# A graph network's update step without row means, its result kept in PSUM, and three more groups of rows copied on the chip

## The chip, the cores and the metric

The kernel runs on one core of one Trainium2 chip. A core has a matrix engine (PE, with its weight loads shown apart as PEld), a vector engine (DVE), an activation engine (ACT), a general engine (POOL) that here issues gathers, and SP, which issues most other DMAs. Each works through its own queue in order; semaphores tie them together. The metric is the device time of one execution in microseconds (us). Three runs of the kernel before the change gave 2449.85, 2456.73 and 2466.41 us; their median is 2456.73 us.

## What is computed

One layer of a message-passing graph network over 12,500 nodes (64 features) and 200,000 edges (32 features, sorted by target node), then a residual and a normalisation of each row:

```python
msg_in = concatenate([nodes[row], nodes[col], edge_features])      # 200000 x 160
messages = relu(msg_in @ mW1 + mb1) @ mW2 + mb2
aggregated = segment_sum(messages, col, num_segments=12500)
upd = relu(concatenate([nodes, aggregated]) @ uW1 + ub1) @ uW2 + ub2
y = x + upd
out = (y - mean(y)) / sqrt(var(y) + 1e-5)                          # over the 64 features
```

Here `row` is the random source of an edge (`src`) and `col` its sorted target (`dst`).

## The kernel before

**Tables and tiles.** The first part of the run computes two tables in DRAM: A, every node's features times the source part of `mW1`, and B, the same for the target part. Edges are worked in tiles of 128; 6 tiles make a step (261 steps), 12 make a super block (131, number g). All values are 32-bit floats.

**One step s** of the main loop is written out by hand; this order is the order of every engine's queue. `edge_part` (L379) multiplies, on PE, a selection matrix and the edge features `l` with `rhs`, which holds a window of 32 rows of B and the weights of the edge features, into PSUM (`pc`, two buffers that rotate). `node_part` adds the gathered rows of A on DVE (L405, or L402) and applies relu on ACT (L406, or L403), giving `h`. One step later `collect` counts the edges per target (`cnt`, L435) and sums `h` per target (`sums`, L438) on PE, both in PSUM over a window that a register names. Every second step, `select` builds on DVE the selection for the next super block: it compares target numbers with first nodes (L250) and with slot numbers (L256). The slot numbers and the first nodes lie in PSUM, in a tile `cps` of 272 columns; the first nodes of 80 super blocks fit and are computed by `first_nodes`.

**Source rows.** For most tiles POOL gathers 128 rows of A by an indirect DMA (L218), up to nine steps ahead (`rows`, nine buffers). For two of the six tiles of some groups, the "copied" ones (a list `COPIED` made from `PACE`, 105 groups), the rows come from the transposed x that lies in SBUF: two tiles' 128 columns are copied one by one, half by ACT (L350, `singly`) and half by DVE (L357, `joined`), and PE multiplies them with the weights (L382). The address of a copy stands in two registers, which the engine loads first (L327), up to 16 words, for 8 columns, at once. The copies of a group are spread over the steps ahead of its own: DVE's share of a step falls into two or three parts (`share`) between its large operations, ACT's into one at the end of the step.

**Updates.** A run of steps whose targets span fewer than 448 nodes makes a period (34 of them, `UPD`). Its `sums` and `cnt` have 480 columns. When it ends, `close` copies them to SBUF (L453 ACT, L452 DVE), `carry` adds the 32 columns of overlap to the next period, `update` multiplies with the weights (`pu`, L475 and L476, in a `pc` buffer), `activated` applies relu (L481, ACT, at the end of the step), and a step later `residual` (L489, L491) computes y = x + update of four blocks of 128 nodes into `py`, which takes a `pc` buffer too. In the following steps, ACT copies y to SBUF (`evacuate`, L497), DVE takes statistics block by block (L505, L507), ACT a square root (L512), DVE a reciprocal and four subtract-and-multiply operations (L518, L521), and SP stores the rows (L529).

Of the kernel before, what the change touches and what calls it, by code (L numbers as in the profile page):

```python
# [10 lines left out]
F32 = mybir.dt.float32  # L11
# [6 lines left out]
P = 128  # L18
# [24 lines left out]
BS = 11  # L43
UB = 4
NCOL = (-(-N // P) + UB) * P
UN = 448
UW = UN + WIN
ONE = D - 1
LS = 8
# [21 lines left out]
U8 = mybir.dt.uint8  # L71
YBASE = XBASE + 4 * XCOLS
LEAD = 8
PACE = ((11, 0.42), (50, 0.446), (130, 0.429), (261, 0))
FINAL = 258


# [26 lines left out]

UPD = updates()

NODES = 80
UL = min(UB * P, -(-int(N * (1 - (UPD[-1] * SUB * P / E) ** 2) + WIN // 2) // 64) * 64)


# [1 line left out]
def gnn_kernel(ctx: ExitStack, tc: tile.TileContext, x1T, x, eT, e_rows, src, src_row, dst, dst_row, wlist, wrow, wnext, whalf,  # L112
# [54 lines left out]
    uz = const.tile([P, DH], F32, name="uz")  # L167
    ub1_s = const.tile([DH, 1], F32, name="ub1_s")
    u2 = const.tile([DH, D], F32, name="u2")
    ux = const.tile([P, D], F32, name="ux")  # L170
    w2u = const.tile([DH, DH], F32, name="w2u")
    ident = const.tile([P, P], F32, name="ident")
# [50 lines left out]
    with tc.tile_pool(name="sup", bufs=2) as sup, tc.tile_pool(name="work", bufs=2) as work, tc.manual_schedule():  # L223
# [13 lines left out]
        def first_nodes(a, b):  # L237

            c = WIN + SUP // 2 * (a % NODES)
            nc.vector.tensor_scalar(cps[:, c:c + SUP // 2 * (b - a)], wh[:, SUP // 2 * a:SUP // 2 * b], pidx, None, op0=ALU.add)  # L240

        def select(g, at=None):


            nt = min(SUP, NT - g * SUP)
            l = L[g]
            c = WIN + SUP // 2 * (g % NODES)
            node = cps[:, c:c + SUP // 2]
# [7 lines left out]
            nc.vector.tensor_tensor(s[:, :nt], slot.unsqueeze(1).broadcast_to([P, nt, WIN]),  # L256
                                    drc[:, g * SUP:g * SUP + nt].unsqueeze(2).broadcast_to([P, nt, WIN]),
                                    op=ALU.is_equal)
            S[g] = s
# [201 lines left out]
        def blocks(u):  # L461
            return UB if u + 1 < K else -(-UL // P)
# [21 lines left out]

        def residual(u):

            py = psum.tile([P, UB, D], F32, name="py", tag="sums" if u + 2 == K else "pc")
            for i in range(blocks(u)):
                nc.tensor.matmul(py[:, i], xw[u % 2][:, i * P:(i + 1) * P], ux, start=i == 0, stop=False)  # L489
            for i in range(blocks(u)):  # L490
                nc.tensor.matmul(py[:, i], hT[:, i * P:(i + 1) * P], u2, start=False, stop=i + 1 == blocks(u))  # L491
            ys[u] = py

        def evacuate(u):

            y = work.tile([P, UB, D], F32, name="y")
            nc.scalar.copy(y, ys[u])  # L497
            ys[u] = y

        def statistics(u):  # L500

            st = work.tile([P, UB, nc.vector.BN_STATS_DIM], F32, name="st")
            mv = work.tile([P, UB, nc.vector.BN_AGGR_DIM], F32, name="mv")
            for i in range(blocks(u)):
                nc.vector.bn_stats(out=st[:, i], in_=ys[u][:, i])  # L505
            for i in range(blocks(u)):
                nc.vector.bn_aggr(out=mv[:, i], in_=st[:, i])  # L507
            mvs[u] = mv

        def deviation(u):  # L510
            sd = work.tile([P, UB], F32, name="sd")
            nc.scalar.activation(sd[:, :blocks(u)], mvs[u][:, :blocks(u), 1], AF.Sqrt, bias=eps)  # L512
            sds[u] = sd

        def norm(u):
            y, mv, sd = ys.pop(u), mvs.pop(u), sds.pop(u)
            rs = work.tile([P, UB], F32, name="rs")
            nc.vector.reciprocal(rs[:, :blocks(u)], sd[:, :blocks(u)])  # L518
            o = work.tile([P, UB, D], F32, name="y") if u + 1 == K else y
            for i in range(blocks(u)):  # L520
                nc.vector.tensor_scalar(o[:, i], y[:, i], mv[:, i, 0:1], rs[:, i:i + 1],  # L521
                                        op0=ALU.subtract, op1=ALU.mult)
            us[u] = (us[u], o)

        ys, mvs, sds = {}, {}, {}
# [153 lines left out]
        def rest(s):  # L679
# [4 lines left out]
                zeros(s - 3, 8)  # L684
            if s == 6:
                first_nodes(8, NODES)
            if s == 2 * NODES - 3:
                first_nodes(NODES, NSUP)
            if s == 9:
                columns_list()  # L690
            if s == 1:
# [35 lines left out]

        def checks():

# [34 lines left out]
        at_end = {n: [(evacuate, K - 3), (statistics, K - 3)], n + 1: [(deviation, K - 3), (norm, K - 3), (store, K - 3)],  # L764
                  n + 2: [(stage, K - 2) for stage in (evacuate, statistics, deviation, norm, store)]}

        period = [max(u for u in range(K) if UPD[u] <= s) for s in range(NSUB)]
        transpose(0)
# [3 lines left out]
        for s in range(last + 2):  # L772
# [48 lines left out]
            if due.get(s) == K - 1:  # L821
                activated(K - 1)
                residual(K - 1)
                statistics(K - 1)
                deviation(K - 1)
            if s + 2 in due and due[s + 2] + 1 < K:
# [15 lines left out]

    flag = nc.values_load(flag_i[0:1, 0:1], min_val=0, max_val=2 * EBULK,
# [167 lines left out]
```

## Time and profile before

| | us |
|---|---|
| median of three runs | 2456.73 |
| lowest, highest | 2449.85, 2466.41 |
| the profiled execution | 2450.92 |
| its span, first to last instruction | 2449.1 |

The profile is of one execution, 0.24% under the median. Its page counts an engine as busy while an instruction works; loading registers, waiting on semaphores and issuing DMAs are not counted, and stand as idle time, either under the name of what ended the wait or as "issue", when nothing visible was waited for. "Remote" is a release that the trace ascribes to no instruction. In the rows of groups the columns are line, engine, operation, output and input, shapes and number; then busy us and mean ns of one; then the idle us just before them and what ended most of it. The granted clock of PE has a mean of 0.555 in this run.

### The profile page before, as it was taken

Reading aid. Unit: us, or ns where it says so; the run is one execution under the profiler, and the core shown is the slowest. Engines: PE = TensorE matmul, PEld = TensorE weight load, DVE = VectorE, ACT = ScalarE, POOL = GpSimd, SP = SyncE. Lnnn points to the kernel's source line nnn. Section 1 sums busy time; section 2 is a strip of 40 time slices with the busy share of each in tenths; the row PEclk is TensorE's granted clock in tenths of the full one; section 3 lists DMA queues with packets and bytes.
Section 4 is the critical chain, followed back from the end, with each engine's and each line's share of the span. In section 5 each row is a group of like instructions: output and inputs, shape, how many; then the busy total and the mean of one; then the engine's idle time right before and its main releaser. Section 6 shows DMA issues by size and latency. Waiting matters only on the chain.

```text
span 2449.1 us, 47549 instructions
## 1 busy us (share of the span) xinstructions
PE 1612.1 (66%) x9656; PEld 1381.8 (56%) x9656; DVE 1125.1 (46%) x7813; ACT 1603.2 (65%) x7158; POOL 1278.5 (52%) x1362
## 2 busy tenths in 40 slices
PE   1247566666657665666666667576667777878878
PEld 1236455555546554655555556565555665656767
DVE  0212544444545444444454454544454454445554
ACT  0005666667877776767776777676777777767773
POOL 7254555555555555555555555555555555545550
PEclk9956555555555555555555555555555555555556
DMA  5343232332222222222222232322222233223332
GB/s 133 102 119 97 75 81 77 83 84 64 75 69 71 74 64 70 72 66 74 69 71 77 71 82 73 80 75 76 78 74 77 73 83 80 72 73 80 81 81 53
DMA packets 207165, 191.50 MB, mean 78 GB/s; under 512 B 57211, under 2 KB 173265, under 8 KB 206881
## 3 DMA queue, kind: packets, MB, share of 16 engines
q0 software_dynamic: 43296, 86.79, 14.3%
q1 hardware_dynamic: 149040, 92.72, 13.7%
q10 hardware_dynamic: 14546, 8.93, 1.3%
q8 instruction: 91, 1.49, 0.3%
q14 instruction: 192, 1.57, 0.2%
HBM read 170.52 MB, written 17.76 MB: 77 GB/s over the span
## 4 chain that ended last, share of the span: by engine, by line
issue 27%; PE 18%; ACT 12%; DVE 12%; POOL 12%; another core or an unknown queue 8%; DMA 3%; DVEq 3%; ACTq 2%; SPq 1%; POOLq 0%
POOL xg L218 12%; ACT xc L350 10%; PE sums L438 7%; DVE xc L357 6%; PE pc L379 6%; DVEq L327 3%; DVE h L405 2%; ACTq L327 2%; PE py L489 1%; PE py L491 1%; DVE pc L402 1%; DVE l L250 1%; SPq L287 1%; DMA xg<-tab_a,src_s 1%
## 5 line engine op out<-in xcount | busy, mean ns | idle before, releaser
L218 POOL DMA_INDIRECT xg<-tab_a,src_s x1293 | 1220.7, 944 | 1086.5 <-DVE h L405 427.7
L350 ACT ACTIVATE xc<-xtop,xbot 128x1 f32 x6720 | 1321.7, 281 | 342.4 <-issue 319.7
L357 DVE TENSOR_TENSOR xc<-xtop,xbot 128x1 int32 x6720 | 608.5, 154 | 723.1 <-issue 701.8
L438 PE MATMUL sums<-sel,h 128*128 128x32 f32 x3126 | 686.1, 385 | 208.9 <-issue 71.5
L438 PEld LDWEIGHTS sums<-sel,h 128*128 128x128 f32 x3126 | 653.4, 312 | 239.1 <-issue 71.6
L379 PE MATMUL pc<-rhs,l 64*128 64x128 f32 x3126 | 477.4, 434 | 284.1 <-issue 77.3
L379 PEld LDWEIGHTS pc<-rhs,l 64*128 64x128 f32 x3126 | 389.4, 307 | 357.5 <-issue 182.6
L435 PEld LDWEIGHTS <-one 128*1 128x1 bf16 x1563 | 63.6, 83 | 219.6 <-issue 209.6
L406 ACT ACTIVATE h<-h 128x768 f32<-128x768 f32 x147 | 121.7, 828 | 83.9 <-DVE h L405 76.5
L405 DVE TENSOR_TENSOR h<-pc,xg 128x768 f32<-128x768 f32 x147 | 139.4, 949 | 65.8 <-PE pc L379 18.8
L435 PE MATMUL cnt<-sel,one 128*1 128x32 bf16 x1563 | 107.5, 188 | 82.3 <-issue 82.0
L250 DVE TENSOR_TENSOR l<-l,cps 128x768 f32<-128x768 int32 (+1 forms) x134 | 127.2, 949 | 67.9 <-DMA l<-in_dst_row 51.5
L403 ACT ACTIVATE h<-pc 128x768 f32<-128x768 f32 x105 | 84.1, 801 | 103.0 <-DVE pc L402 84.3
L402 DVE TENSOR_TENSOR pc<-pc,xg 128x512 f32<-128x512 f32 x105 | 73.4, 699 | 146.4 <-remote 57.9
L256 DVE TENSOR_TENSOR sel<-cps,drc 128x384 f32<-128x384 f32 x131 | 72.0, 549 | 113.3 <-PE sums L438 75.6
L382 PE MATMUL pc<-w1a,xc 64*128 64x128 f32 x420 | 89.5, 405 | 6.9 <-issue 6.9
L382 PEld LDWEIGHTS pc<-w1a,xc 64*128 64x128 f32 x420 | 79.1, 317 | 8.2 <-issue 8.1
L594 ACT COPY tb<-pb 128x512 f32<-128x512 f32 (+1 forms) x13 | 7.4, 569 | 114.0 <-remote 73.6
L584 PE MATMUL pb<-w1a,xtop 64*128 64x128 f32 x100 | 23.5, 413 | 86.7 <-DVE tb L592 62.0
L489 PE MATMUL py<-ux,xw 128*128 128x64 f32 x268 | 62.4, 410 | 27.3 <-remote 22.1
L489 PEld LDWEIGHTS py<-ux,xw 128*128 128x128 f32 x268 | 56.6, 311 | 34.9 <-remote 23.0
L433 PE MATMUL cnt<-zero_b 128*1 128x480 bf16 x34 | 18.6, 547 | 81.2 <-DVE xw L452 47.4
(103 smaller groups left out, 844.3 us busy)
## 6 DMA issues: line engine op xcount, KB each, us to landing
l<-in_dst_row SPq DMA_DIRECT2D x262, 96.0 KB
l<-in_eT SPq DMA_DIRECT2D x262, 96.0 KB
xg<-tab_a,src_s POOLq DMA_INDIRECT x1293
rhs<-tab_b SPq DMA_DIRECT2D x361, 32.0 KB
tab_b<-tb SPq DMA_DIRECT2D x13, 512.0 KB
rhs<-tab_b SPq DMA_DIRECT2D x387, 16.0 KB
tab_a<-tb ACTq DMA_DIRECT2D x12, 512.0 KB
out<-y SPq DMA_DIRECT2D x33, 128.0 KB
```

What stands on the lines that cost most here:

```text
L218: nc.gpsimd.indirect_dma_start(out=a[:, i, :] if s < XG else a[:, i // 2, i % 2, :], out_offset=None, in_=A[:, :] if s >= XG else x[:, :], ...
L250: nc.vector.tensor_tensor(l[r], l[r].bitcast(I32), node[r].unsqueeze(2).broadcast_to([r.stop - r.start, SUP // 2, P]), op=ALU.is_equal)
L327: _, v = nc.values_load_multi_w_load_instructions(col_a[k % P:k % P + 1, k // P].rearrange("k e b -> k (e b)")[:, 2 * a:2 * m], engines=[e ...
L350: nc.scalar.activation(o[:, e:e + 1], top.bitcast(F32), AF.Identity, bias=bot.bitcast(F32))
L357: nc.vector.tensor_tensor(o[:, e:e + 1].bitcast(I32), top.bitcast(I32), bot.bitcast(I32), op=ALU.bitwise_or)
L379: nc.tensor.matmul(pc[:, b, k, :], L[g][q:q + 64, m, :], rhs[g % 2][q:q + 64, w, :], start=s >= XG or k == 0, stop=s >= XG and not copied)
L382: nc.tensor.matmul(pc[:, b, k, :], xc[s][q:q + 64], w1a[q:q + 64], start=False, stop=True)
L405: nc.vector.tensor_tensor(h[:, b, :m], pc[:, b, :m], a[:, b, :m], op=ALU.add)
L406: nc.scalar.activation(h[:, b, :m], h[:, b, :m], AF.Relu)
L435: nc.tensor.matmul(pn[:, bass.ds(ws[i], WIN)], one, SB[g][:, k0 + i, :, 1], start=False, stop=ends and i == n - 1)
L438: nc.tensor.matmul(ps[:, bass.ds(ws[i], WIN)], h[:, i % 2, i // 2, :], S[g][:, k0 + i, :], start=False, stop=ends and i == n - 1)
L489: nc.tensor.matmul(py[:, i], xw[u % 2][:, i * P:(i + 1) * P], ux, start=i == 0, stop=False)
```

## The change

Five things change together.

- **No row means.** The weights behind y, `u2` and `ux`, get each row's mean over the 64 outputs subtracted (into `u2c` and `ux`, once, on DVE), so that y has a mean of zero in every row. Statistics shrink to a sum of squares.
- **y stays in PSUM.** `residual` writes into a fixed part of the tile `cps` (now 384 columns: 32 slot numbers, 96 first nodes, 256 for y) in place of a `pc` buffer. ACT's copy goes; ACT writes the squares to SBUF instead, at the end of the step of the residual, one step before the copy stood. DVE sums them with one reduction in place of eight statistics operations, ACT takes the root of the scaled sum, and one multiplication on DVE, reading y from PSUM, replaces four operations. Every stage and the store come one step earlier. First nodes of 32 super blocks fit; `select` computes the next ones when they are used up.
- **DVE's copies by whole loads.** `share` splits a step's copies at multiples of four pairs of columns, so that parts begin with full loads of 16 words.
- **Updates of 480 nodes.** `UN` is 480, sums and counts have 512 columns, and there are 32 periods.
- **108 copied groups.** `PACE` rises from 0.446 to 0.459 between steps 50 and 130 and from 0.429 to 0.442 after.

```diff
-UN = 448
+UN = 480
-PACE = ((11, 0.42), (50, 0.446), (130, 0.429), (261, 0))
+PACE = ((11, 0.42), (50, 0.459), (130, 0.442), (261, 0))
-NODES = 80
+NODES = 32
+YC = WIN + NODES * SUP // 2
...
-    cps = cpool.tile([P, WIN + NODES * SUP // 2], F32, name="cps")
+    cps = cpool.tile([P, YC + UB * D], F32, name="cps")
...
+            if g and g % NODES == 0:
+                first_nodes(g, min(g + NODES, NSUP))
...
         def share(todo, part, of):
-            n = -(-len(todo) // of)
-            todo = todo[part * n:part * n + n]
+            c = CHUNK // 2
+            n = max(int(len(todo) / of / c + 0.5), 1) * c
+            todo = todo[part * n:(part + 1) * n if part + 1 < of else None]
...
         def residual(u):
-            py = psum.tile([P, UB, D], F32, name="py", tag="sums" if u + 2 == K else "pc")
+            py = cps[:, YC:].rearrange("p (i d) -> p i d", d=D)
...
-                nc.tensor.matmul(py[:, i], hT[:, i * P:(i + 1) * P], u2, start=False, stop=i + 1 == blocks(u))
+                nc.tensor.matmul(py[:, i], hT[:, i * P:(i + 1) * P], u2c, start=False, stop=i + 1 == blocks(u))
...
-        def evacuate(u):
-            y = work.tile([P, UB, D], F32, name="y")
-            nc.scalar.copy(y, ys[u])
-            ys[u] = y
+        def squares(u):
+            n = blocks(u)
+            sq = work.tile([P, UB, D], F32, name="y")
+            nc.scalar.activation(sq[:, :n], ys[u][:, :n], AF.Square)
+            sqs[u] = sq
...
         def statistics(u):
-            for i in range(blocks(u)):
-                nc.vector.bn_stats(out=st[:, i], in_=ys[u][:, i])
-            for i in range(blocks(u)):
-                nc.vector.bn_aggr(out=mv[:, i], in_=st[:, i])
+            nc.vector.tensor_reduce(ss[:, :n], sqs.pop(u)[:, :n], AX.X, ALU.add)
...
-            nc.scalar.activation(sd[:, :blocks(u)], mvs[u][:, :blocks(u), 1], AF.Sqrt, bias=eps)
+            nc.scalar.activation(sd[:, :n], ss[:, :n], AF.Sqrt, bias=eps, scale=1.0 / D)
...
-            for i in range(blocks(u)):
-                nc.vector.tensor_scalar(o[:, i], y[:, i], mv[:, i, 0:1], rs[:, i:i + 1],
-                                        op0=ALU.subtract, op1=ALU.mult)
+            nc.vector.tensor_tensor(o[:, :n], y[:, :n], rs[:, :n].unsqueeze(2).broadcast_to([P, n, D]), op=ALU.mult)
...
+            for i, (v, w) in enumerate(((u2, u2c), (ux, ux))):
+                mean = work.tile([P, 1], F32, name=f"mean{i}", bufs=1)
+                nc.vector.tensor_reduce(mean, v, AX.X, ALU.add)
+                nc.vector.tensor_scalar(mean, mean, 1.0 / D, None, op0=ALU.mult)
+                nc.vector.tensor_scalar(w, v, mean, None, op0=ALU.subtract)
...
-            for stage, n in ((evacuate, 2), (statistics, 3), (deviation, 4), (norm, 5)):
+            for stage, n in ((statistics, 2), (deviation, 3), (norm, 4)):
...
             singly(s, 0, 1)
+            if earlier(1) is not None and earlier(1) + 3 < K:
+                squares(earlier(1))
...
-            if earlier(5) is not None:
-                store(earlier(5))
+            if earlier(4) is not None:
+                store(earlier(4))
```

More of the change, by code (lines that the diff above doesn't have):

```diff
@@ L169, in gnn_kernel @@
     u2 = const.tile([DH, D], F32, name="u2")
+    u2c = const.tile([DH, D], F32, name="u2c")
     ux = const.tile([P, D], F32, name="ux")
@@ L510, in deviation @@
+        sqs = {}
+        def statistics(u):
+            n = blocks(u)
+            ss = work.tile([P, UB], F32, name="ss")
+            nc.vector.tensor_reduce(ss[:, :n], sqs.pop(u)[:, :n], AX.X, ALU.add)
+            mvs[u] = ss
         def deviation(u):
+            n, ss = blocks(u), mvs.pop(u)
             sd = work.tile([P, UB], F32, name="sd")
-            nc.scalar.activation(sd[:, :blocks(u)], mvs[u][:, :blocks(u), 1], AF.Sqrt, bias=eps)
+            nc.scalar.activation(sd[:, :n], ss[:, :n], AF.Sqrt, bias=eps, scale=1.0 / D)
@@ L513, in deviation @@
             sds[u] = sd
         def norm(u):
-            y, mv, sd = ys.pop(u), mvs.pop(u), sds.pop(u)
+            n, y, sd = blocks(u), ys.pop(u), sds.pop(u)
             rs = work.tile([P, UB], F32, name="rs")
-            nc.vector.reciprocal(rs[:, :blocks(u)], sd[:, :blocks(u)])
-            o = work.tile([P, UB, D], F32, name="y") if u + 1 == K else y
-            for i in range(blocks(u)):
-                nc.vector.tensor_scalar(o[:, i], y[:, i], mv[:, i, 0:1], rs[:, i:i + 1],
-                                        op0=ALU.subtract, op1=ALU.mult)
+            nc.vector.reciprocal(rs[:, :n], sd[:, :n])
@@ L523, in norm @@
+            o = work.tile([P, UB, D], F32, name="y")
+            nc.vector.tensor_tensor(o[:, :n], y[:, :n], rs[:, :n].unsqueeze(2).broadcast_to([P, n, D]), op=ALU.mult)
             us[u] = (us[u], o)
@@ L686, in rest @@
                 first_nodes(8, NODES)
-            if s == 2 * NODES - 3:
-                first_nodes(NODES, NSUP)
             if s == 9:
@@ L763, in gnn_kernel @@
         n = UPD[K - 1]
-        at_end = {n: [(evacuate, K - 3), (statistics, K - 3)], n + 1: [(deviation, K - 3), (norm, K - 3), (store, K - 3)],
-                  n + 2: [(stage, K - 2) for stage in (evacuate, statistics, deviation, norm, store)]}
+        at_end = {n: [(squares, K - 3), (statistics, K - 3)], n + 1: [(deviation, K - 3), (norm, K - 3), (store, K - 3)],
+                  n + 2: [(stage, K - 2) for stage in (squares, statistics, deviation, norm, store)]}
         period = [max(u for u in range(K) if UPD[u] <= s) for s in range(NSUB)]
@@ L823, in gnn_kernel @@
                 residual(K - 1)
+                squares(K - 1)
                 statistics(K - 1)
```

3 lines of the change are left out of this document (removed).

## The prediction

> **What bounds the kernel now.** I read the page first (engines, chain), then the busy time by stretch, then each engine's waits in those stretches, the groups of instructions, and last the timeline around one update.
>
> ```profile
> span 2449.1 us, 47549 instructions
> PE 1612.1 (66%) x9656; PEld 1381.8 (56%) x9656; DVE 1125.1 (46%) x7813; ACT 1603.2 (65%) x7158; POOL 1278.5 (52%) x1362
> issue 27%; PE 18%; ACT 12%; DVE 12%; POOL 12%; another core or an unknown queue 8%; DMA 3%; DVEq 3%; ACTq 2%; SPq 1%; POOLq 0%
> ```
>
> No engine is above 66% and the chain of what ended last belongs to nobody: 27% of it is "issue", time in which nothing visible is waited for. An average says little here, so the stages are taken apart. Between 600 and 1900 us the loop runs over steps 52 to 195 (counted by L379's products); after that updates come every three to five steps.
>
> ```profile
> core 0: us, PE busy (x) PEld busy (x) DVE busy (x) ACT busy (x) POOL busy (x), PEclk, DMA share, GB/s
> 600.00:1900.00 1300.00, 859.61 (x5078) 739.16 (x5078) 638.29 (x4643) 941.48 (x4327) 707.26 (x750) 0.52 0.27 73
> 1900.00:2400.00 500.00, 390.20 (x2102) 322.76 (x2102) 251.36 (x1817) 356.01 (x1634) 263.23 (x279) 0.54 0.30 77
> ```
>
> ACT's waits in the first of these stretches ("us in total, times, longest"):
>
> ```profile
> ACT xc L350 <- issue: 225.5, 330, 2.0
> ACT y L497 <- remote: 49.7, 7, 10.7
> ACT sums_s L453 <- remote: 23.6, 5, 6.5
> ACT h L403 <- DVE pc L402: 18.7, 13, 3.3
> ACT y L497 <- PE pc L379: 8.4, 1, 8.4
> ...
> ACT h L406 <- DVE h L405: 6.7, 12, 1.1
> ```
>
> Busy 941.5 us and "issue" before its copies 225.5 us fill 1167 of 1300 us. Only 33.8 us (18.7 + 8.4 + 6.7) are waits for another engine's work. In this middle stretch ACT is the engine that everything else follows. In the stretch behind it, ACT waits:
>
> ```profile
> ACT h L403 <- DVE pc L402: 51.6, 19, 3.8
> ACT h L406 <- DVE h L405: 37.8, 25, 3.2
> ACT xc L350 <- issue: 25.5, 59, 1.1
> ACT y L497 <- PE pc L379: 13.2, 2, 7.5
> ```
>
> Here 102.6 us of 500 (51.6 + 37.8 + 13.2) are spent waiting for DVE and PE, so ACT has room. POOL never sets the pace; over the whole run it waits for DVE to give row buffers back:
>
> ```profile
> POOL xg L218 <- DVE h L405: 427.7, 115, 13.4
> ```
>
> So the six gathers that the three newly copied groups save are worth nothing by themselves: POOL would only wait longer.
>
> **The change part by part.** The durations:
>
> ```profile
> L350 ACT ACTIVATE xc<-xtop,xbot 128x1 f32 x6720 | 1321.7, 281 | 342.4 <-issue 319.7 <-DMA ub_s<-in_ub 17.5
> L357 DVE TENSOR_TENSOR xc<-xtop,xbot 128x1 int32 x6720 | 608.5, 154 | 723.1 <-issue 701.8 <-DMA xg<-tab_a,src_s 6.2 <-remote 1.8
> L405 DVE TENSOR_TENSOR h<-pc,xg 128x256 f32<-128x256 f32 x1 | 0.4, 424 | 0.3 <-PE pc L379 0.3
> L481 ACT ACTIVATE hTu<-pu,ub_s 128x448 f32<-128x448 f32 x33 | 20.4, 618 | 12.0 <-PE pu L476 8.0 <-remote 3.0 <-issue 0.8
> L453 ACT COPY sums_s<-sums 128x480 f32<-128x480 f32 x34 | 18.6, 548 | 33.7 <-remote 24.8 <-PE pc L382 5.5 <-PE sums L438 3.4
> L497 ACT COPY y<-py 128x256 f32<-128x256 f32 x33 | 12.0, 364 | 80.2 <-remote 49.7 <-PE pc L379 21.6 <-PE py L491 8.4
> L512 ACT ACTIVATE sd<-mv,eps 128x4 f32<-128x4 f32 x33 | 9.4, 285 | 1.0 <-DVE mv L507 0.9
> L505 DVE BATCH_NORM_STATS2 st<-y 128x6 f32<-128x64 f32 x132 | 20.0, 212 | 5.9 <-ACT y L497 3.0 <-issue 2.9
> L507 DVE BATCH_NORM_AGGREGATE mv<-st 128x2 f32<-128x6 f32 x134 | 12.2, 153 | 0.0
> L521 DVE TENSOR_SCALAR y<-y,mv,rs 128x64 f32<-128x64 f32 x132 | 33.6, 326 | 22.6 <-remote 19.2 <-DVE rs L518 2.5
> ```
>
> *108 copied groups.* Counts here are of the two programs as built. ACT makes 6912 copies for 6720, with 1009 register loads for 986. A copy costs 1321.7/6720 = 0.197 us of ACT, a load leaves about 319.7/986 = 0.324 us idle. None of the additions lies before step 50; steps 50 to 195 get 122 copies and 13 loads, 24.0 + 4.2 = +28.2 us; later steps get 70 copies and 10 loads, 17.0 us, under ACT's 102.6 us of waits there. If that cover were gone, they would cost these 17 us.
>
> *Fewer, wider updates.* 32 for 34. In the middle stretch 17 become 15; behind it there are 16 either way. One costs ACT 0.548 + 0.618 + 0.364 + 0.285 = 1.815 us, so −3.6 us. The wider ones add 32 of 480 columns to L453 (+0.037) and 32 of 448 to L481 (+0.044): 15 × 0.081 = +1.2 us. PE's work on the 480 columns is nearly what it was on 448 in more updates.
>
> *Squares by ACT.* A 128x256 read of PSUM takes the place of a 128x256 read of PSUM; I give Square the Copy's 0.364 us. It stands one step earlier, at the end of ACT's step behind its copies. L497's wait in the middle stretch was 49.7 us "remote" in seven pieces. One of them:
>
> ```profile
> 763.07 0.37 ACT L497 COPY y<-py 128x256 f32<-128x256 f32 x1 [8.23 <-remote]
> ```
>
> What the move saves is between 0 and 49.7 us; a wait that is met earlier is mostly met again, so I take −15, nearer to zero.
>
> *Statistics and scaling on DVE.* Per update (20.0 + 12.2 + 33.6)/33 = 1.99 us disappears. A reduction of 128x256 and a multiplication of 128x256 come instead. No row shows either; the nearest is L405 on 128x256, 0.424 us each; a lower bound is L521's 0.326. So 0.65 to 0.85, taken 0.85: −1.1 us an update, about −18 us in each stretch. In the middle ACT's own work covers this (DVE is not last). Behind 1900 us, where ACT waits for DVE, a third counts: −6.
>
> *DVE's whole loads.* DVE's loads fall from 1143 to 1036.
>
> ```profile
> L327 DVEq TENSOR_LOAD <-col_a x1143: 344/885/2525, 223.5 to 2397.8; - x191
> ```
>
> ```profile
> L327 DVEq TENSOR_LOAD <-col_a x2: 345/720/1095, 750.6 to 752.0; - x2
> ```
>
> The rows give minimum, median and maximum in ns, of all and of two that follow each other. The second is one load of 16 words (1095 ns) and one of 4 (345 ns): 62.5 ns a word and 95 ns a load. The words grow (2 a copy, +384). So the loads change by +24.0 − 10.2 = +13.8 us, not by −107 whole loads; the 192 copies add 192 × 608.5/6720 = +17.4. With the statistics DVE comes out at about −5 us over the run. The other bound prices a load by count, 701.8/1143 = 0.614 us, −65.7 us: a rival below. What does help: in a step with a select, 4 words and two copies go behind L250 and again behind L256, each some 0.5 us; the select, for whose end the next edge features wait, starts 0.5 us sooner. Behind 1900 us, 32 times: 0 to −16, taken −6.
>
> *y out of the matmul ring.* Two `pc` buffers rotate; `py` took one once per update, so an edge product had to wait until the step before it was added up. PE's waits there: middle stretch, then behind it:
>
> ```profile
> PE pc L379 <- ACT h L403: 18.1, 8, 6.3
> ```
>
> ```profile
> PE pc L379 <- DVE h L405: 6.5, 3, 4.7
> ```
>
> In the middle PE follows ACT anyway (0); later 0 to −6.5, taken −5.
>
> *y in the bank of slot numbers.* The tile `cps` now holds slot numbers, first nodes and y. As built, the residual's first matmul waits for the select (L256) where both fall in one step, 13 times, with the counts and sums of the step behind it on PE; squares wait likewise. One update's timeline now:
>
> ```profile
> 2302.51 1.97 PE L489 MATMUL py<-ux,xw 128*128 128x64 f32 x8
> ...
> 2305.84 0.55 DVE L256 TENSOR_TENSOR sel<-cps,drc 128x384 f32<-128x384 f32 x1
> ...
> 2306.37 2.77 PE L438 MATMUL sums<-sel,h 128*128 128x32 f32 x12
> ...
> 2310.04 1.74 PE L379 MATMUL pc<-rhs,l 64*128 64x128 f32 x11 [0.90 <-issue]
> ```
>
> Today `py` starts at 2302.51, the select ends at 2306.39: the new wait is 3.9 us here. PE idles 0.9 us before the next edge product, so 3.0 us may get through. In the middle PE's waits for ACT cover it; behind 1900 us six such updates cost 0 to +18, taken +8. [...]
>
> First nodes are computed four times instead of once in the middle, under 1 us each on DVE; the mean-free weights cost a few small DVE operations once. Both nothing.
>
> **Sum.** Middle: +28.2 − 3.6 + 1.2 − 15 = +11. Behind: −6 − 6 − 5 + 8 = −9. Together +2 us on the profiled execution's 2450.92 us. That lies 5.8 us (0.24%) below the median 2456.73; put on the median it is 2459.
>
> **The rivals.**
>
> *DVE paces the middle as much as ACT, and a load costs by count.* For it: DVE's idle 701.8 us before copies, more than any other row; ACT's in-order copies may only look saturated. Against it: the 62.5 ns a word, and ACT's 33.8 us of waits. Then the middle loses 69 loads (−42), gains 122 copies (+11), loses −18 of statistics: −49, of which at most the 33.8 us that ACT waits for others can show. With −9 behind: −43, 2414.
>
> *The shared bank (slower).* One mechanism: PE's residual queues behind the select, 13 times; it decides once PE has less than 3 us of slack when it reaches the residual. All uncovered: 13 × 3.0 = 39 instead of the +8: 2490. For it: the timeline above. Against: in the middle PE waits for ACT right afterwards. [...]
>
> *ACT's copies in full.* The squares' wait comes back and DVE's savings stay hidden: +28.2 − 3.6 + 1.2 = +26, 2483. For it: ACT's rows in the middle. It needs nothing but that −15 and −9 fail to appear.
>
> That the change does not do what it says is ruled out: 108 groups, 32 updates and 1036 loads stand in the built program.
>
> **How the numbers follow.** What a measurement of this kernel tells from no change is about 1%: under 2432, over 2481. Forecast (within 1%) 0.42, its own range 2440 to 2480, made of the squares' wait (up to 15 more, or 15 less) and the small terms behind 1900 us. DVE by count, 0.32: faster. Shared bank 0.14 and ACT in full 0.12: slower. The range must hold 8 in 10 and signs differ, so it spans from the DVE rival's 2414 with a little beyond to the bank's 2490 and ten more: 2410 to 2500. Faster 0.32, same 0.42, slower 0.26.
>
> **What would show it.** Right: ACT busy plus "issue" again fills the middle stretch, its busy time there up by about 20 us; the squares' row waits less than L497's 80.2 us; the new reduction and product near 0.42 us. Bank: a wait of `py`'s first matmul, or of the squares, on the select, totalling over 25 us, and PE's sums late behind it. DVE by count: idle before DVE's copies down by over 50 us and the middle shorter. The prediction is wrong altogether if the stretches in which engines wait for nothing visible (the "issue" rows, single waits of up to 2.0 us on ACT) become fewer or more for a reason that no count above holds: I price them as unchanged.

## The result, and the profile after

The changed kernel took 2497.92 us (median of four runs, 2491.79 to 2498.91), the kernel before 2459.20 us beside it: a ratio of 1.0154, 95% interval 1.0115 to 1.0194. That is slower by more than the 1% that this kernel's measurement can tell. The time lies inside the predicted range, at its upper end and 39 us above the forecast of 2459; slower had been given 0.26. The range reached that far for the rival of the shared bank (2490 us and ten more), not for anything in the sum.

The page of the changed kernel, span and engines:

```profile
span 2490.0 us, 47360 instructions
PE 1609.1 (65%) x9616; PEld 1377.5 (55%) x9616; DVE 1090.9 (44%) x7668; ACT 1643.7 (66%) x7343; POOL 1273.6 (51%) x1356
```

ACT is busy 40.5 us longer (1603.2 before), DVE 34.2 us less (1125.1). The groups of instructions of the same run (busy us, mean ns of one, then the idle us ahead of them and what ended it). L355 and L362 are the copies of ACT and DVE that were L350 and L357; L494 is the residual's first product, L503 the squares, L512 the reduction, L526 the scaling:

```profile
L355 ACT ACTIVATE xc<-xtop,xbot 128x1 f32 x6912 | 1365.5, 281 | 388.6 <-issue 364.4 <-DMA tab_b<-tb 17.7
L362 DVE TENSOR_TENSOR xc<-xtop,xbot 128x1 int32 x6912 | 609.6, 154 | 689.8 <-issue 676.7 <-DMA xg<-tab_a,src_s 1.9 <-DVE h L410 0.9
...
L494 PE MATMUL cps<-ux,xw 128*128 128x64 f32 x252 | 59.8, 415 | 34.1 <-DVE sel L260 24.2 <-DVE xc L362 6.5 <-issue 3.4
L526 DVE TENSOR_TENSOR y<-cps,rs 128x256 f32<-128x256 f32 (+1 forms) x32 | 13.5, 420 | 40.3 <-remote 36.9 <-DVE rs L524 2.5
L512 DVE TENSOR_REDUCE ss<-y 128x4 f32<-128x256 f32 (+1 forms) x32 | 13.2, 411 | 55.9 <-ACT y L503 41.6 <-issue 14.2
L503 ACT ACTIVATE y<-cps 128x256 f32<-128x256 f32 (+1 forms) x32 | 12.0, 375 | 89.4 <-remote 31.2 <-PE pc L384 20.1 <-PE cps L496 19.3
```

The residual's first product in the kernel before, for comparison:

```profile
L489 PE MATMUL py<-ux,xw 128*128 128x64 f32 x268 | 62.4, 410 | 27.3 <-remote 22.1 <-issue 3.6 <-DVE h L405 1.4
```

Four things are to be seen. The idle time before ACT's copies named "issue" rose from 319.7 to 364.4 us, 44.7 us, more than the whole span grew (40.9). The squares wait 89.4 us where the copy of y waited 80.2: coming a step earlier saved nothing. DVE's reduction, which stands ahead of the select in DVE's queue, waits 55.9 us, most of it for the squares; the statistics it replaces had waited 5.9 us. And the residual's first product waits 34.1 us where it had waited 27.3, but for something new: all 12 of its waits end within 0.06 us of the select's end, also those that the row gives to another line, while in the kernel before no wait ended so.

The row of y's copy hides something that matters below. In the kernel before, the piece that the prediction shows reads as follows (start, duration, idle time before in brackets):

```profile
748.49 1.91 PE L491 MATMUL py<-u,hTu 128*128 128x64 f32 x8
...
753.99 0.84 ACT L406 ACTIVATE h<-h 128x768 f32<-128x768 f32 x1 [0.42 <-issue]
...
757.11 0.37 PE L379 MATMUL pc<-rhs,l 64*128 64x128 f32 x1 [2.59 <-issue]
...
759.91 0.37 PE L379 MATMUL pc<-rhs,l 64*128 64x128 f32 x1 [2.43 <-issue]
...
763.07 0.37 ACT L497 COPY y<-py 128x256 f32<-128x256 f32 x1 [8.23 <-remote]
```

The product that the copy needs ended at 750.40, and still the copy started 12.7 us later, while PE too started one product per 2.4 to 2.8 us. Over the whole run, 68.9 of the copy's 80.2 us pass with its product already ended by over 0.2 us; only 11.3 us are time in which y was not there yet. Of the squares' 89.4 us in the changed kernel, 53.8 us pass so and 35.6 us are a wait for y.

What "issue" is here, the timeline of the changed kernel shows (the same columns):

```profile
1003.06 0.94 POOL L220 DMA_INDIRECT xg<-tab_a,src_s  x1 [0.30 <-issue]
1004.31 0.94 POOL L220 DMA_INDIRECT xg<-tab_a,src_s  x1 [0.30 <-issue]
1004.39 0.16 DVE L362 TENSOR_TENSOR xc<-xtop,xbot 128x1 int32 x1 [1.24 <-issue]
1004.40 0.29 ACT L355 ACTIVATE xc<-xtop,xbot 128x1 f32 x1 [1.11 <-issue]
1005.11 0.16 DVE L362 TENSOR_TENSOR xc<-xtop,xbot 128x1 int32 x1 [0.55 <-issue]
1005.56 0.94 POOL L220 DMA_INDIRECT xg<-tab_a,src_s  x1 [0.30 <-issue]
1005.79 0.84 ACT L411 ACTIVATE h<-h 128x768 f32<-128x768 f32 x1 [1.09 <-issue]
```

For some microseconds ACT and DVE start one instruction per 0.7 or 1.4 us, though the profile shows no wait, while POOL goes on at its own pace, 0.94 us a gather and 0.30 us between two. I call these the slow stretches. The time in which ACT and DVE both stand in a gap over 0.3 us that is named "issue" adds up to 200.6 us in the kernel before and 219.3 us in the changed one.

By the starts of DVE's additions (L402 and L405, now L407 and L410), one a step, the two profiled runs differ by +6.9 us from step 10 to 50 (366.1 to 373.0), +21.8 us from 50 to 196 (1293.4 to 1315.2) and +10.1 us from 196 to 258 (544.1 to 554.2). The prediction had 0, +11 and -9.

### The profile page after: what moved, and what is told of

It reads as the page before. It is cut to its first block, busy times and chain, and to the rows that moved or that the text cites. A ratio compares the mean times of both kernels' runs of the same rounds, so it can differ in the third digit from the quotient of the medians.

```text
span 2490.0 us, 47360 instructions
## 1 busy us (share of the span) xinstructions
PE 1609.1 (65%) x9616; PEld 1377.5 (55%) x9616; DVE 1090.9 (44%) x7668; ACT 1643.7 (66%) x7343; POOL 1273.6 (51%) x1356
## 3 DMA queue, kind: packets, MB, share of 16 engines
q1 hardware_dynamic: 147828, 92.48, 13.5%
## 5 line engine op out<-in xcount | busy, mean ns | idle before, releaser
L220 POOL DMA_INDIRECT xg<-tab_a,src_s x1287 | 1215.8, 945 | 1130.5 <-DVE h L410 462.3
L355 ACT ACTIVATE xc<-xtop,xbot 128x1 f32 x6912 | 1365.5, 281 | 388.6 <-issue 364.4
L362 DVE TENSOR_TENSOR xc<-xtop,xbot 128x1 int32 x6912 | 609.6, 154 | 689.8 <-issue 676.7
L384 PE MATMUL pc<-rhs,l 64*128 64x128 f32 x3126 | 477.1, 437 | 237.0 <-issue 61.0
L410 DVE TENSOR_TENSOR h<-pc,xg 128x768 f32<-128x768 f32 x144 | 136.6, 949 | 89.7 <-remote 26.0
L407 DVE TENSOR_TENSOR pc<-pc,xg 128x512 f32<-128x512 f32 x108 | 75.5, 699 | 138.8 <-remote 93.4
L260 DVE TENSOR_TENSOR sel<-cps,drc 128x384 f32<-128x384 f32 x131 | 71.8, 548 | 124.2 <-PE sums L443 60.4
L494 PE MATMUL cps<-ux,xw 128*128 128x64 f32 x252 | 59.8, 415 | 34.1 <-DVE sel L260 24.2
L494 PEld LDWEIGHTS cps<-ux,xw 128*128 128x128 f32 x252 | 54.2, 316 | 41.7 <-DVE sel L260 26.6
L503 ACT ACTIVATE y<-cps 128x256 f32<-128x256 f32 (+1 forms) x32 | 12.0, 375 | 89.4 <-remote 31.2
```

What stands on the lines that cost most here:

```text
L220: nc.gpsimd.indirect_dma_start(out=a[:, i, :] if s < XG else a[:, i // 2, i % 2, :], out_offset=None, in_=A[:, :] if s >= XG else x[:, :], ...
L355: nc.scalar.activation(o[:, e:e + 1], top.bitcast(F32), AF.Identity, bias=bot.bitcast(F32))
L362: nc.vector.tensor_tensor(o[:, e:e + 1].bitcast(I32), top.bitcast(I32), bot.bitcast(I32), op=ALU.bitwise_or)
L384: nc.tensor.matmul(pc[:, b, k, :], L[g][q:q + 64, m, :], rhs[g % 2][q:q + 64, w, :], start=s >= XG or k == 0, stop=s >= XG and not copied)
L410: nc.vector.tensor_tensor(h[:, b, :m], pc[:, b, :m], a[:, b, :m], op=ALU.add)
```

## The experiments

**Two kinds of chip.** The times of these runs can't be read without this: on three chips the kernel before took 1713 to 1714 us, on two others 2465 to 2492 us, much as on the chip of the prediction. I call them quick and long chips. Every ratio below is to the kernel before on the same chip in the same set of runs. The four long rows come from several chips and sets, and on one long chip the kernel before itself took 2464.6 us in one set (u10's) and 2482.2 us in another (u11's), 0.7% apart; differences of that size between long rows are weaker than their intervals look.

| run | left out or added | kind | ratio | 95% interval |
|---|---|---|---|---|
| first | the whole change | long | 1.0154 | 1.0115 to 1.0194 |
| u9 | whole, y alone in its bank | long | 1.0079 | 1.0048 to 1.0110 |
| u10 | whole, 92 copied groups | long | 1.0179 | 1.0144 to 1.0213 |
| u11 | whole without the part on y | long | 1.0040 | 1.0020 to 1.0061 |
| u5 | the whole change | quick | 0.9979 | 0.9967 to 0.9991 |
| u6 | the kernel before again | quick | 1.0003 | 0.9991 to 1.0016 |
| u1 | whole, 105 copied groups | quick | 1.0005 | 0.9994 to 1.0015 |
| u2 | whole, 448 nodes | quick | 1.0014 | 0.9999 to 1.0029 |
| u3 | whole, old division of DVE's copies | quick | 1.0034 | 1.0021 to 1.0047 |
| u4 | whole without the part on y | quick | 1.0011 | 1.0001 to 1.0021 |
| u7 | whole, 12 gathers more | quick | 1.0051 | 1.0034 to 1.0068 |
| u8 | 108 groups alone | quick | 1.0076 | 1.0059 to 1.0093 |
| u12 | as u9, stages a step later | quick | 1.0236 | 1.0221 to 1.0252 |

**One part undone at a time.** Four kernels; the first three change the changed kernel, the fourth the kernel before.

```diff
-PACE = ((11, 0.42), (50, 0.459), (130, 0.442), (261, 0))
+PACE = ((11, 0.42), (50, 0.446), (130, 0.429), (261, 0))
```

> The changed kernel with the old 105 copied groups; the rest of the change stays. Its time is compared with the kernel before (2459 us) and the changed kernel (2498 us, ratio 1.015). Theory A (the 122 more copies and 13 more loads of ACT between steps 50 and 195 are paid in full, nothing else matters): 24 to 28 us come back, some 2472 us, ratio 1.004 to 1.007. Theory B (y in the bank of the slot numbers and the new order of squares, reduction and select around each update): less than 8 us come back, ratio 1.012 to 1.017, and the wait of the residual's first product for the select stays at some 24 us. Theory C (wider updates or the new division of DVE's copies): as B here.

```diff
-UN = 480
+UN = 448
```

> The changed kernel with updates of 448 nodes (34 of them) in place of 480 (32); the rest stays. Theories A and B: the two more updates cost ACT 3.6 us in the middle and B's waits occur two more times, so 2498 to 2508 us, ratio 1.015 to 1.020. Theory C (the wider sums and counts, or where the updates now fall between the steps, cost the time): down by 10 us or more, ratio below 1.011.

```diff
-            c = CHUNK // 2
-            n = max(int(len(todo) / of / c + 0.5), 1) * c
-            todo = todo[part * n:(part + 1) * n if part + 1 < of else None]
+            n = -(-len(todo) // of)
+            todo = todo[part * n:part * n + n]
```

> The changed kernel with the old division of a step's copies on DVE; the rest stays. DVE's loads go back up by over 60 of few words. Theories A and B: within 8 us of the changed kernel (ratio 1.012 to 1.019), rather above it. Theory C (the new division puts copies ahead of operations that are waited for): down by 10 us or more, ratio below 1.011. Loads priced by count, as the prediction's rival had it: up by 20 us or more, ratio above 1.023.

The fourth takes the three edits above into the kernel before, and nothing of the part on y.

> The kernel before with 108 copied groups, updates of 480 nodes and the new division of DVE's copies, but with row means, y copied to SBUF by ACT two steps behind the update's end, and the old statistics. Theory A: the part on y is worth nothing or a gain of some 10 us, so 2495 to 2510 us, ratio 1.015 to 1.021. Theory B: the whole loss is in the part on y, so 2455 to 2470 us, ratio 0.998 to 1.005. Half and half: 2475 to 2485 us.

All four came from a quick chip, within 0.4% of the kernel before: neither A's 28 us nor B's 20 us of loss is there to be undone. The next two ask whether the change loses anything on such a chip, and for profiles.

> The changed kernel as it is, beside the kernel before on one chip. In the first four experiments the kernel before took 1714 us, where it took 2459 us in the runs of the prediction, and its variants lay between 1.0005 and 1.0034 of it. Theory F (the extra 740 us were slow dispatch, which is not the kernel's, and the 1.5% are lost only where dispatch is slow): where the kernel before takes some 1714 us, the ratio is 1.000 to 1.004; where it takes some 2460 us, 1.012 to 1.019. Theory A (ACT's additional copies in full): +28 us either way, ratio 1.011 to 1.017. Theory B (bank and order around each update): +20 to +39 us either way, ratio above 1.011.

> The kernel before, for a profile from the same chip as the changed kernel's. Ratio 1.000. Where it takes some 1714 us: theory F expects ACT's idle time named issue ahead of its copies to be under 30 us (319.7 us in the runs of the prediction) and SP's register moves near 0.03 us each; theories A and B say nothing of it.

The changed kernel is 0.2% faster there, 1709.29 against 1713.53 us. The loss belongs to the long chips alone, as theory F had it, though 0.9979 is a little under the 1.000 that F gave. The page of the kernel before on a quick chip:

```profile
span 1712.2 us, 47549 instructions
PE 1448.5 (85%) x9656; PEld 1245.9 (73%) x9656; DVE 1092.6 (64%) x7813; ACT 1534.8 (90%) x7158; POOL 1280.4 (75%) x1362
...
L218 POOL DMA_INDIRECT xg<-tab_a,src_s x1293 | 1221.5, 945 | 394.1 <-issue 363.6
L350 ACT ACTIVATE xc<-xtop,xbot 128x1 f32 x6720 | 1273.2, 284 | 28.4 <-issue 17.6
```

Its register loads for ACT (minimum, median and maximum in ns, and a count of those back to back):

```profile
L327 ACTq TENSOR_LOAD <-col_a x986: 308/1024/2122, 136.5 to 1656.3; - x198
```

And the waits of POOL in the changed kernel there (us in total, times, longest):

```profile
POOL xg L220 <- issue: 385.2, 1264, 0.3
POOL xg L220 <- DMA xg<-tab_a,src_s: 9.8, 32, 0.3
POOL xg L220 <- DVE xc L362: 7.3, 24, 0.3
POOL xg L220 <- DVE h L410: 2.1, 7, 0.3
```

The same 986 loads take the same median of 1024 ns, and yet ACT's copies stand only 17.6 us in "issue" instead of 319.7: the loads run beside the copies, and what the prediction had charged to them was the slow stretches. Gaps over 0.3 us named "issue" on ACT and DVE at once add up to 6.2 us here, against 200.6 on the long chip, and the copy of y waits 6.6 us in all, never more than 0.2 us after its product ended. Without the slow stretches, POOL has no wait over 0.3 us once it has begun; it gathers without a break from start to end. Its last gather and what remains behind it, from the traces (us):

| kernel on a quick chip | gathers | last gather ends | span | behind it |
|---|---|---|---|---|
| before | 1353 | 1694.3 | 1712.2 | 17.9 |
| whole change | 1347 | 1687.3 | 1706.6 | 19.3 |
| whole, 105 copied groups | 1353 | 1698.9 | 1718.5 | 19.5 |
| whole, 448 nodes | 1347 | 1689.9 | 1708.2 | 18.3 |
| old division of DVE's copies | 1347 | 1686.3 | 1718.0 | 31.6 |
| without the part on y | 1347 | 1687.6 | 1713.1 | 25.5 |
| 12 gathers more | 1359 | 1703.1 | 1725.0 | 21.9 |
| 108 groups alone | 1347 | 1686.6 | 1717.2 | 30.6 |
| u12 | 1347 | 1736.6 | 1754.7 | 18.1 |

Two of these rows come from a test of this reading: 12 gathers more in the changed kernel, and the 108 groups alone in the kernel before.

```diff
-        return tiles(s)[:SUB - 2 * (s in COPIED)]
+        return tiles(s)[:SUB - 2 * (s in COPIED) + (s in COPIED[20:104:7])]
```

> The changed kernel with 12 gathers more: in 12 of the copied steps the fifth tile's rows are gathered too, into a place that nothing reads. ACT, DVE and PE do what they did. Where the kernel before takes some 1714 us (POOL's row there has no wait but 0.3 us of issue between gathers of 0.95 us), theory P (POOL paces) expects 12 x 1.25 = +15 us, ratio 1.005 to 1.009; theory A (ACT paces) expects no change from the changed kernel, ratio 0.997 to 0.999. Where the kernel before takes some 2460 us, both expect no change, ratio 1.012 to 1.019.

> The kernel before with 108 copied groups and nothing else of the change. ACT makes 192 copies more (36 us at one per 0.185 us), POOL 6 gathers fewer. Where the kernel before takes some 1714 us: theory P expects 6 x 1.25 = -7.5 us where nothing is in the way, ratio 0.995 to 0.998; theory A +28 to +36 us, ratio 1.016 to 1.021; both engines full: between, 0.998 to 1.006. Where it takes some 2460 us: theory A expects +28 to +45 us, ratio 1.011 to 1.018, theory B (bank and order) less than +8 us, ratio below 1.004.

Twelve gathers moved the last gather by 15.8 us (1703.1 less 1687.3; 15 expected) and the ratio by 0.72%: on a quick chip POOL paces. The groups alone end the gathers 7.7 us sooner, but what is left behind the last one grows by 12.7 us (17.9 to 30.6), since ACT and DVE, with 192 copies more each, fall behind (steps 50 to 196 take 926.2 us there and 907.4 before). The profiled run is the fastest of that kernel's four, 1718.97 us where their median is 1725.58; over all runs the ratio is 1.0076. That is above the 1.006 given for both engines full, and far below A's 1.016. The other parts bring the remainder back to 19.3, the division most (31.6 without it).

**On long chips.** Here the loss could be taken apart.

```diff
-    cps = cpool.tile([P, YC + UB * D], F32, name="cps")
+    yps = cpool.tile([P, UB * D], F32, name="yps")
+    cps = const.tile([P, YC], F32, name="cps")
...
-            py = cps[:, YC:].rearrange("p (i d) -> p i d", d=D)
+            py = yps.rearrange("p (i d) -> p i d", d=D)
```

> The changed kernel with slot numbers and first nodes in SBUF, so that y has its bank of PSUM to itself and the residual's first product no longer waits for the select, nor the next select for the product behind it. Where the kernel before takes some 1714 us (the wait of that product for the select is 13.7 us in 10 pieces in the changed kernel's profile there): the wait disappears; theory P (POOL's gathers end at the same time, only the tail behind them can shorten) expects at most 2 us, ratio 0.996 to 0.999; theory B (the bank's wait is on the path) 6 to 14 us, ratio 0.990 to 0.995. If DVE's two selects are slower from SBUF (0.944 and 0.545 us each from PSUM), the ratio goes above 0.999. Where it takes some 2460 us: theory B 20 to 39 us back, ratio 1.000 to 1.007; theory A none, ratio 1.011 to 1.019.

The groups of u9 (its L495, L513 and L504 are L494, L512 and L503 above):

```profile
L495 PE MATMUL yps<-ux,xw 128*128 128x64 f32 x252 | 59.5, 412 | 2.4 <-issue 2.4
...
L513 DVE TENSOR_REDUCE ss<-y 128x4 f32<-128x256 f32 (+1 forms) x32 | 13.2, 414 | 67.1 <-ACT y L504 44.6 <-issue 22.5
L504 ACT ACTIVATE y<-yps 128x256 f32<-128x256 f32 (+1 forms) x32 | 11.9, 373 | 96.6 <-PE pc L385 41.2 <-remote 39.6 <-PE yps L497 7.6
```

The residual's wait fell from 34.1 to 2.4 us, and the ratio from 1.0154 to 1.0079: half the loss went with the shared bank, a little less than B's number. That the two belong together is likely but not proven, since the ratios come from two chips and the edit does a second thing: DVE's comparisons now read both operands from SBUF, and POOL's gathers of A's rows take 980 ns instead of 945 (below), which here POOL's own waits can take up (479.4 us for DVE's addition alone). The reduction still waits 67 us, most of it for the squares.

```diff
-PACE = ((11, 0.42), (50, 0.459), (130, 0.442), (261, 0))
+PACE = ((11, 0.38), (50, 0.38), (130, 0.38), (261, 0))
```

> The changed kernel with 92 copied groups (a rate of 0.38 throughout) in place of 108: ACT and DVE make 1024 copies fewer each, POOL 32 gathers more. Where the kernel before takes some 1714 us: theory P (POOL paces) expects 26 gathers more than the kernel before, 26 x 1.25 = +32 us, and a tail behind the last gather of some 18 us, ratio 1.016 to 1.020; theory A (ACT paces) less than the kernel before. Where it takes some 2460 to 2490 us (POOL waits there): theory A (ACT's copies in full, 0.237 us from one to the next there) expects 832 copies fewer than the kernel before, 832 x 0.237 = -197 us at most, and at least the -98 us of half of it, ratio 0.92 to 0.96; theory D (slow dispatch holds all engines but POOL alike, and fewer copies only shift the wait to PE) expects -20 to -60 us, ratio 0.976 to 0.992; theory B (bank and order alone) +20 to +39 us, ratio 1.008 to 1.016.

No theory but B had this one, and B's 1.016 is passed. ACT and DVE lost 1024 copies each, and the kernel is no faster. The page of u10:

```profile
span 2518.7 us, 44856 instructions
PE 1614.5 (64%) x9552; PEld 1377.8 (55%) x9552; DVE 1005.4 (40%) x6644; ACT 1460.7 (58%) x6319; POOL 1302.7 (52%) x1388
...
L355 ACT ACTIVATE xc<-xtop,xbot 128x1 f32 x5888 | 1181.1, 282 | 447.7 <-issue 427.5
...
L260 DVE TENSOR_TENSOR sel<-cps,drc 128x384 f32<-128x384 f32 x131 | 72.1, 550 | 216.9 <-remote 131.0
L503 ACT ACTIVATE y<-cps 128x256 f32<-128x256 f32 (+1 forms) x32 | 12.1, 379 | 182.0 <-remote 99.4
```

ACT's busy time fell by 183 us against the changed kernel, its "issue" before copies rose by 63 and the waits of squares and select by 185 together (182.0 − 89.4 and 216.9 − 124.2). On PE, gaps over 0.3 us named "issue" grew from 289 to 394 us. On these chips ACT is not what the rest follows.

u11 is the kernel of u4 once more.

> Once more the kernel before with 108 copied groups, updates of 480 nodes and the new division of DVE's copies, but with row means and y copied by ACT; it took 1.0011 of the kernel before where that took 1714 us. Asked is a chip on which the kernel before takes some 2460 to 2490 us, where taking 1024 copies from ACT and from DVE brought nothing, which leaves the part on y, the wider updates and the division. Theory B (y's part: its bank, and the order of squares, reduction and select): the loss is gone, ratio 0.996 to 1.006. Theory C (wider updates or the division): it stays, ratio 1.010 to 1.020. Theory D (the slow dispatch takes what it takes, and its stretches vary from build to build by 1% or more): anywhere between, without relation to what is left out.

This time it met a long chip, and most of the loss is gone: 1.0040, as B had it. D's "anywhere between" allows this number too, and no second long run of the whole change tells how far a build's ratio moves by itself. Its rows for the old path of y:

```profile
L490 PE MATMUL py<-ux,xw 128*128 128x64 f32 x252 | 58.6, 408 | 5.5 <-remote 3.9 <-issue 1.4
L506 DVE BATCH_NORM_STATS2 st<-y 128x6 f32<-128x64 f32 x124 | 19.2, 212 | 8.1 <-issue 4.9 <-ACT y L498 3.1
L498 ACT COPY y<-py 128x256 f32<-128x256 f32 x31 | 11.3, 364 | 54.8 <-remote 49.6 <-PE pc L380 2.3 <-PE py L492 1.7
...
L351 ACT ACTIVATE xc<-xtop,xbot 128x1 f32 x6912 | 1366.0, 281 | 379.1 <-issue 355.3 <-DMA wb<-in_wnext 17.0
```

PE's, DVE's and ACT's waits on this path are 68.4 us (5.5 + 8.1 + 54.8), where the changed kernel has 179.4 (34.1 + 55.9 + 89.4). The sum is no price, though: the kernel before has 113.4 (27.3 + 5.9 + 80.2) and is the faster one, and 50.3 of the 54.8 us before the copy pass with its product ended. "Issue" before ACT's copies is 355.3 here too, so that row alone doesn't tell the two apart.

The last run was to split the second half of the loss off: y alone in its bank, and the squares and the reduction each a step apart again.

```diff
-            for stage, n in ((statistics, 2), (deviation, 3), (norm, 4)):
+            for stage, n in ((squares, 2), (statistics, 3), (norm, 4)):
...
-            if earlier(1) is not None and earlier(1) + 3 < K:
-                squares(earlier(1))
+            if earlier(3) is not None:
+                deviation(earlier(3))
```

> The changed kernel with y alone in its bank, and with the stages behind the residual put back by a step as far as y's buffer allows: the squares behind the relu of the next step, the reduction on DVE a step after them, the root at the end of that step. Where the kernel before takes some 2460 to 2490 us: y alone in its bank had left 1.0079, with the reduction still waiting 67 us for the squares ahead of the select (8 us for the statistics in the kernel with the old y, which had 1.0040). Theory B2 (the other half of the loss is that wait): the reduction waits less than 15 us and the ratio is 0.998 to 1.005. Theory B1 (only the bank mattered): 1.005 to 1.011. Where it takes some 1714 us: theory P (POOL's gathers set the end, the tail behind them is already as short as in the kernel before) expects what the changed kernel has, 0.996 to 1.000, by either.

It met a quick chip, so it says nothing of the second half, and it missed by 2.4%. The groups of u12:

```profile
L221 POOL DMA_INDIRECT xg<-tab_a,src_s x1287 | 1263.7, 982 | 392.4 <-issue 363.1 <-DMA xg<-tab_a,src_s 13.5 <-DVE xc L363 6.7
```

A gather takes 982 ns instead of 946, and 1347 of them 49 us more: the last gather ends at 1736.6 instead of 1687.3. The cause lies in u9's edit, which u12 keeps (u9's gathers take 980 ns too). Those gathers that overlap the select's first comparison take 1160 ns (213 of them), the others 949; in u9 1176 ns (172) and 950; in the changed kernel on a quick chip, where that comparison reads first nodes from PSUM, 948 and 946. 213 × 0.21 is 45 of the 49 us.

## Why the prediction was right and wrong

**The terms of the sum.** Without y the prediction's terms are 28.2 − 3.6 + 1.2 − 6 = +20 us; u11 has 0.40%, some +10 us. The terms of y are −15 − 6 − 5 + 8 = −18 us; the first ratio less u11's is 1.14%, +28 us (17 to 39 from the two intervals, on two chips of one kind). The part on y is where the forecast failed, by some 46 us, a little more than the 39 us that it missed; the rest of the sum was some 10 us too high and hid a part of that by luck. u11 and the first result share 108 groups, the updates and the division, so that the loss lies with y's part is measured, as far as two long chips can be compared; the pieces below are in part argued.

- *"What the move saves is between 0 and 49.7 us ... so I take −15"*: this step failed. The 49.7 us were no wait for y: in all seven pieces the residual's last product had ended 7.0 to 14.7 us before the copy started, and for 40.0 of these 49.7 us DVE too stood in gaps over 0.3 us named "issue". The slow stretches held the copy up, and the earlier place in the queue did not save that. The squares wait 89.4 us (the copy 80.2), of which the time without y grew from 11.3 to 35.6 us. And a wait that the sum did not hold came with it: the reduction ahead of the select on DVE, 55.9 us against 5.9. The stages moved a step earlier on every engine, and only ACT's wait was counted. That the reduction's wait is the second half of the loss (1.0079 to 1.0040) is argued from the rows and was not tested.
- *The shared bank, +8, as a rival +39*: the wait is shown, 12 times (13 expected) and 34.1 us, all ending with the select, and it passes the 25 us that the prediction named as the mark; the row's 24.2 us is only the part that the profile gives to the select by name. One of the twelve, 8.1 us, is long because the select itself had stood idle for 7.6 us. What it costs lies between, 0.75% or 18 us (6 to 31), if the two chips can be compared and u9's slower gathers cost nothing. Whether y and the slot numbers have to wait for each other in one bank no run shows; measured is the wait of 34.1 us with both in the tile `cps`, and 2.4 us, none of it for the select, with y alone (u9). The rival's 2490 us was the nearest of all to the 2498 measured.
- *"In this middle stretch ACT is the engine that everything else follows"*, and *"a load leaves about 319.7/986 = 0.324 us idle"*: both failed. The signs that the prediction asked for were there:

```profile
600.00:1900.00 1300.00, 845.47 (x5009) 729.23 (x5005) 609.88 (x4512) 953.79 (x4386) 693.36 (x735) 0.52 0.27 71
```

  The fourth number with a count, ACT's busy time between 600 and 1900 us, is up by 12.3 us from 941.48 (20 expected). They proved nothing: with 1024 copies fewer on ACT nothing is gained on a long chip (u10), and on a quick chip the same loads leave 17.6 us idle, 0.018 us each. Busy time plus "issue" filled ACT's stretch, but "issue" was no work of ACT's. And "Only 33.8 us ... are waits" left out 73.3 us of "remote" (49.7 + 23.6) in the same list. The rival "ACT's copies in full" rested on the same rows and fell with them, though its 2483 us was nearer than the forecast; that was luck.
- *"I price them as unchanged"*, of the stretches without a visible wait: they did change, 319.7 to 364.4 us before ACT's copies, and in u10 they took up freed time.
- *Loads by words*: right in the size of the loads. They took 983.3 us before and 996.8 after, +13.5 where +13.8 was expected, and "issue" before DVE's copies fell by 25 us, less than the 50 that would have shown the rival "DVE by count". That rival's 2414 us fell. The −6 for an earlier select was not tested by itself.
- *Statistics*: a reduction is 0.411 us and a product 0.420, priced at 0.424 each. On the long chip the reduction's wait grew by 50 us, more than the 39 us by which DVE's work on y shrank (65.8 to 26.7).
- *y out of the ring*: not settled. The idle time before edge products fell from 284.1 to 237.0 us, but it is 267.2 in u9, with y out of the ring too, and 268.9 in u11, with y in it.
- *"POOL never sets the pace"*: right on a long chip, where it waits 462.3 us for DVE's addition in the changed kernel (427.7 before), wrong on a quick one, where six gathers fewer end the gathers 7.0 us sooner and, with the other parts keeping the remainder short, bring the gain of 4.2 us (the six alone, in u8, brought none).

What stays open: why ACT and DVE stand in such gaps on long chips (200.6 us at once against 6.2), what of u11's 0.4% is due to which part, whether the old order of stages with slot numbers left in PSUM would bring the rest back, and how far the long ratios move from set to set without any change. On long chips no version tried beats the kernel before; on quick ones the changed kernel does.

## What to carry to other kernels

Before a row named "issue" is charged to the instruction beneath it, ask whether other engines show such gaps at the same time. Here ACT and DVE did, for 200.6 us; the 0.324 us a load taken from that row were 0.018 on a quick chip, and 1024 copies fewer on ACT bought nothing (u10, 1.0179). Before a wait is priced as saved, look whether what it waits for had ended long before. Here it had, by 7.0 to 14.7 us, and the earlier place in the queue saved nothing (89.4 us of waits, 80.2 before). When a stage is moved a step, list what stands behind its consumers on every engine, here the select behind the reduction (55.9 us of waits, 5.9 before), and not only the wait of the stage itself. When small operands are moved out of PSUM, look at the mean duration of a second engine's instructions: here POOL's gathers went from 946 to 982 ns, and the last of them ended 49 us later (u12 beside u5).

## What the runs showed of the hardware

- The long chips' traces lack records. Of the kernel before, the prediction's trace has 15,193 records of semaphore changes by instructions and 10,893 by DMAs; from a quick chip, 42,370 and 36,456. Waits that end with "remote" stand in the long traces alone (509 us in the kernel before, none on the quick chip), which fits the missing records. Register moves on SP take 29 ns at the median in both, but 131 of 820 take over 0.4 us on the long chip, and none over 0.05 us on the quick one. The durations of copies, loads and gathers are nearly the same (ACT's copies 281 and 284 ns, its loads 1024 and 1024 at the median, gathers 944 and 945). Why records are missing and why instructions start slowly, and whether the one has to do with the other, no run here tested; that POOL keeps its 0.94 us a gather and 0.30 us between two in the slow stretches would have to be explained as well.
- POOL's gathers took longer beside a DVE comparison with both operands in SBUF: 1160 ns for those that overlap it and 949 for the others in u12 (1176 and 950 in u9), where those beside the same comparison with first nodes in PSUM took 948 and the others 946 (u5).
